# A two-layer graph network on one Trainium2 core: the last groups of the second layer in steps of their own, a first layer drained in smaller portions, and three stores moved behind the tables

## The chip, the cores and the metric

The kernel runs on one core of one Trainium2 chip. The metric is the device time of one execution in microseconds (us). A core has five engines that each run their own list of instructions: PE (TensorE, matrix products; its loads of weights are listed as PEld), DVE (VectorE), ACT (ScalarE), POOL (GpSimd) and SP (SyncE). They wait for each other through semaphores. In this kernel SP only starts DMA transfers, and POOL only starts indirect ones: gathers of rows, and a few scattered stores at the end.

## The reference, cut to what matters

There are 6250 nodes with 256 features and 200000 edges, sorted by destination; each edge has 128 attributes.

```python
# layer 1
e = edge_attr @ W_edge + b_edge
msg = relu(x[src] + e)
agg = segment_sum(msg, dst)
h = relu((x + agg) @ W1 + b1) @ W2 + b2
h = relu((h - mean(h, 0)) * rsqrt(var(h, 0) + 1e-5) * gamma + beta)   # statistics over all nodes
x = layernorm(x + h)
# layer 2: attention with 4 heads
z = einsum('nd,hdf->nhf', x, W)
e = leaky_relu((z . a_src)[src] + (z . a_dst)[dst], 0.01)
e = where(e == 0, -1000, e)
ex = exp(e - segment_max(e, dst)[dst])
out = segment_sum(ex / segment_sum(ex, dst)[dst] * z[src], dst)
x = layernorm(x + out)
```

The statistics of layer 1 run over all nodes, so all of layer 1 must be done before the middle part starts, and the gathers of layer 2 read a table that the middle part writes.

## The kernel before, in words

The edges are cut into 1563 tiles of 128, and these into G = 112 groups: 111 groups of 14 tiles and the last, number 111, of 9 tiles. A group covers at most 128 destination nodes, so sums over edges are matrix products with one-hot matrices (a row for each edge, a column for each node of the group). The program is a straight line: Python loops write out every instruction, and within a manual schedule the order written is the order in which DVE, PE, ACT and SP run their lists. There is no planner.

**Layer 1** (to about 2389 us) goes through 782 pairs of tiles. For pair k it starts the gather of pair k+3 on POOL (L658), adds gathered rows to the products of edge attributes (`sums`, DVE, L672), splits the relu into two parts (`upper`, ACT, L677; `lower`, DVE, L681) and adds pair k-2 into its group's accumulator on PE (`add_up`, L691). When a group's last pair has been added, a generator `flush` takes the group out: `totals` (L526 to L545: add the nodes' own features, two transposes on PE, the copy `hw` on ACT, a carry to the next group), then `mlp` (L408 to L424: product, relu on ACT, product, copies of `h2T` on ACT) and `part_stats` (L433 to L442: masked sums `pmk` on DVE, squares on ACT). Even groups below 110 do only `totals`; the odd ones then run one `mlp` for two groups. Groups 110 and 111 have one each. Each `yield` of the generator gives a number of pairs to wait before its next stage is written; `drive` (L729) moves the active generators once in each step. A negative number means that the next stage may only go when its group is the oldest active one. From group 109 on (`hurry`) `drive` writes two stages in each step instead, without waits. What is still active after the last pair is driven to its end, and then the statistics are merged (L503, L470).

**Middle** (2389 to 2467 us): 14 chunks of nodes, the first of 384, then 512 each, and two of 128. For each chunk: normalise, relu, add x (`add_x`, L860 on; it then stores the features `hn` to `hT_tab`, L863, on SP), products, and `tables_out`, which stores the rows that layer 2 gathers (`z_tab`, L926, SP). `dst_table` stores a second table, `ed_tab` (L933, SP), in two halves, the second at the very end. The buffers of the middle part, those of `hn` among them, are given back before layer 2; layer 2's `ring` lies in that space.

**Layer 2** (2467 to 4965 us) is a loop over steps i (L1243). A step starts the gather of group i+1 (POOL, L1022), loads for group i+3 (L1032, L1034, SP), a load of a group's features (`load_h`, L1047, SP), and then weaves several groups at different ages:

- `logits(i)` (L1102 on, DVE): scans of group i's logits, whose ends go to PE as transposes (`tr`).
- `rows_between` (L1120 on, DVE): maxima across rows of edges, then transposes (`bk`) on PE.
- `maxima` (L1138 on, DVE, then exp on ACT, `exs`, L1145).
- `weigh` for each pair of tiles: `y` on DVE (L1159) and products with the one-hots into `acc` on PE (L1163).
- `onehots` (L1080, L1086, ACT) and `places` with `dst_parts` (ACT, PE) for groups to come.
- `leave` in five stages: transposes of the features; a copy `ag` of `acc` (ACT, L1177); the carry added to `acc` (DVE, L1186) with the first part of the normalising; statistics of the row; the rest and the store of `out` (SP, L1202; for the last KT groups a scatter on POOL, L1204).

The gathered rows live in a ring of five groups, so the gather of group g can only start when `y` of group g-5 has been made. Which groups are weighed in step i is said by `summed(i)`: i-2 up to the step `turn`; i-2 and i-1 together in step `turn + 1`; i-1 after it. Here `SHORT = 7`, so `turn` is 105 and the double step is 106. A step has the groups of `summed(i - 1)` leave and makes the one-hots of `summed(i + 1)`. Step 111 has an order of its own (L1268 on), and steps 112 and 113 finish the weighing and the leaving of group 111.

Of the kernel before, what the change touches and what calls it, by code (L numbers as in the profile page):

```python
# [35 lines left out]
LOOK = 3  # L36
RING = 5
YB = 8
SHORT = 7
XTB = 4  # L40
FIRST = 384
CH = 512
# [12 lines left out]
def gnn(ctx, tc, io, N, E):  # L55
    nc = tc.nc
    NSUB = -(-E // P)
    gs = group_starts(NSUB)
    G = len(gs) - 1
# [451 lines left out]
    with ExitStack() as st:  # L511
# [38 lines left out]
        room = [0, False]  # L550
# [143 lines left out]
        K = len(pairs_)  # L694
# [4 lines left out]
        with tc.manual_schedule(engines={ET.DVE, ET.PE, ET.Activation, ET.SP}):  # L699
            def run(gen):  # L700
                for _ in gen:
                    pass

            run(positions(0, ldp))
            pieces(0)
            bias_rows(gp.tile([P, TB * D], F32, tag="xr", name="row", bufs=LEAD + (not wide)))
            run(hot(0))
            load_rest()
            XW[0] = window(0)
            if G > 1:  # L710
                pieces(1)

            side = [positions(r, ldp) for r in range(1, len(parts))]
            rest = [first_table()]
            checks = [order(r, ldp) for r in range(len(parts))]
            hots, active, extras = iter(()), [], []
            fill = zeros()
            for f in range(min(LOOK, K)):
                fetch(f)
                features(f)  # L720

            def step(queue):
                while queue:
                    if next(queue[0], True) is None:
                        return True
                    queue.pop(0)
                return False

            def drive(k, hurry):  # L729

                for a in list(active):
                    if k >= a[0] and (a[2] > 0 or active[0] is a):
                        a[2] = next(a[1], 0)
                        if hurry and a[2] > 0 and k < K:
                            a[2] = next(a[1], 0)
                        if a[2] == 0:
                            active.remove(a)
                        else:
                            a[0] = k + (1 if hurry else abs(a[2]))
                            if a[2] < 0:  # L740
                                a[2] = -1

            for k in range(K + 2):
                g = pairs_[min(k, K - 1)][0]
                hurry = room[1] = g >= G - 3
                if k < K and pairs_[k][1] == 0:
                    hots = hot(g + 1) if g + 1 < G else iter(())
                    if g + 2 < G:
                        pieces(g + 2)
                    else:  # L750
                        ahead()
                    if g + 1 < G:
                        XW[g + 1] = window(g + 1)
                    if g == GB - 1:
                        while step(rest):
                            pass
                j = k - firsts_[g] if k < K else 99
                if k + LOOK < K:
                    fetch(k + LOOK)
                if k < K:  # L760
                    sums(k)
                    upper(k)
                    if 1 <= k:
                        lower(k - 1)
                elif k == K:
                    lower(k - 1)
                if k + LOOK < K:
                    features(k + LOOK)
                if k >= 2:
                    add_up(k - 2)  # L770
                    if k - 2 in lasts_:
                        gg = pairs_[k - 2][0]
                        active.append([k + (1 if hurry else 4), flush(gg, ACC.pop(gg), XW.pop(gg)), 1])
                if k == min(2, K - 1):
                    places_rest()
                if k == (31 if G > 8 else 1):
                    run(fill)
                elif 2 <= k < 31 and k % 3:
                    next(fill, None)
                if j >= 1 and k >= 3:  # L780
                    next(hots, None)
                if k < K and pairs_[min(k + 1, K - 1)][0] != g:
                    run(hots)
                drive(k, hurry)
                if room[0]:
                    room[0] -= 1
                    if extras and next(extras[0], True) is not None:
                        extras.pop(0)
                        room[0] = 0
                if len(side) >= len(parts) - 1 or not rest:  # L790
                    step(side)
                if 2 <= k < K and k % 2 == 0:
                    step(rest)
                if g >= GB:
                    step(checks)
                if k < K and g == TG and pairs_[k][1] == 0:
                    while step(side):
                        pass
                    while step(checks):
                        pass  # L800
                    extras = [tables(pps, wk), break_columns(), break_rows(pps, wk)]
                    extras += [place_rows(t0, pps, wk) for t0 in range(0, NSUB, P)]
                    room[0] = 0
                if k == K - 1:
                    ahead()
                if k >= K - 19:
                    next(early, None)
            run(early)
            while active:
                k += 1  # L810
                drive(k, True)
            for q in (side, rest, checks, extras):
                while step(q):
                    pass
# [3 lines left out]
    def middle(h2T, stats, ahead=()):  # L818

        with ExitStack() as st:  # L820
# [38 lines left out]
            def add_x(ci):  # L859
                c0, c1 = cs[ci]  # L860
                hn = M["hn", ci][:, :, :c1 - c0]
                nc.vector.tensor_tensor(hn, hn, M.pop(("xt", ci)), op=OP.add)
                nc.sync.dma_start(hT[:, :, c0:c1], hn)  # L863

            def square(ci, k):
                c0, c1 = cs[ci]
# [61 lines left out]
            def dst_table(b0, b1):  # L928

                e7 = zp.tile([P, b1 - b0, EW], F32, name=f"e7_{b0}")  # L930
                nc.vector.tensor_copy(e7[:, :, EW - 1], r_all[:, b0:b1])
                split3(e7.bitcast(BF16)[:, :, :3 * H].rearrange("p b (h c) -> p b h c", c=3), e_all[:, b0:b1], zp)
                nc.sync.dma_start(ed_tab[b0 * P:b1 * P].rearrange("(b p) d -> p b d", p=P), e7)  # L933

            nch = len(cs)
            half = nch // 2

            def at(f, i, *args):
# [3 lines left out]
            with tc.manual_schedule(engines={ET.DVE, ET.PE, ET.Activation, ET.SP}):  # L942
# [13 lines left out]
                for i in range(nch + 3):  # L956
# [16 lines left out]
                    if i - 3 == half:  # L973
                        dst_table(0, cs[half][1] // P)
                dst_table(cs[half][1] // P, NB)

    rest_ = ExitStack()
    rest_.enter_context(tc.manual_schedule(engines={ET.DVE, ET.PE, ET.Activation, ET.SP}))
# [4 lines left out]
    with ExitStack() as st:  # L983
# [228 lines left out]


        turn = max(0, G - SHORT)

        def among(gg):
            return [g for g in gg if 0 <= g < G]

        def summed(i):
            return among([i - 2] if i <= turn else [i - 2, i - 1] if i == turn + 1 else [i - 1])  # L1220

        def run(gen):
            for _ in gen:
# [8 lines left out]
        with tc.manual_schedule(engines={ET.DVE, ET.PE, ET.Activation, ET.SP}):  # L1232
# [10 lines left out]
            for i in range(G + 2):  # L1243
                work = summed(i)
                units = [(g, *u) for g in work for u in pairs(g)]
                hots = [onehots(g) for g in summed(i + 1)]
                outs = [leave(g) for g in summed(i - 1) if ("acc", g) in T]
                parts_, spots = iter(()), []
                if i + 1 < G:
                    gather(i + 1)  # L1250
# [2 lines left out]
                    spots = [places(i + 3)]  # L1253
                if i < G:
                    load_pen(i)
                for g in work:
                    load_h(g)
                    maxima(g)
                if i + 2 < G:
                    parts_ = dst_parts(i + 2)  # L1260
# [4 lines left out]
                        if parts:  # L1265
                            next(parts_, None)

                if i == G - 1 and i > turn + 1:  # L1268

                    some(2)  # L1270
                    logits(i)
                    step(outs)
                    step(hots)
                    some(2)
                    step(hots)
                    rows_between(i)
                    step(outs)
                    some(1)
                    step(hots)
                    step(outs)  # L1280
                    while units or hots:
                        some(1)
                        step(hots)
                    step(outs)
                    out = outs
                    continue
                while out:
                    step(out)
                if i + 1 < G:
                    breaks(i + 1)  # L1290
                step(outs)
                for g in among([i - 1] if i <= turn else []):
                    rows_between(g)
                step(spots)
# [19 lines left out]
                some(1)  # L1314
                while outs:
                    step(outs)
                while units or hots:
                    some(1)
                    step(hots)
                    if len(work) > 1 and not out and len(units) < 4 and ("acc", work[0]) in T:  # L1320
                        out = [leave(work[0])]
                    step(out)
# [221 lines left out]
```

## Time and profile before

| what | value |
|---|---|
| median of 7 runs | 4987.55 us (4973.74 to 4994.21) |
| the runs | 4973.74, 4974.01, 4978.93, 4987.55, 4988.18, 4988.72, 4994.21 |
| the profiled execution's own time | 4977.61 us |
| its span | 4975.8 us, 1.8 us less than its time |
| PE, DVE, ACT, POOL busy | 61%, 55%, 53%, 60% of the span |
| last gather of layer 1; merge of statistics | 2339.2 us; 2389.1 us |
| first gather of layer 2; end of the last gather | 2467.6 us; 4895.7 us |
| last store | 4964.39 us, 0.99 us long |

The span runs from the first instruction to the last in the trace of one execution; times in the trace are counted from its start. A row such as `L1022 POOL DMA_INDIRECT ring<-z_tab,src_sb x1563` names the line of the kernel, the engine, the operation, what is written from what, and how often. In the timeline the first two columns are the start and the busy time in us; a bracket gives the idle time of the engine just before the instruction and the instruction that ended it. The clock given is the one granted to PE, as a share of full speed.

### The profile page before, as it was taken

The numbers are of one execution on the slowest core, as the hardware profiler recorded it, in microseconds if no ns is written. First come the engines' busy times: TensorE is split into PE (matmuls) and PEld (weight loads), VectorE is DVE, ScalarE is ACT, GpSimd is POOL, SyncE is SP. The second block draws the span as 40 slices with busy tenths as digits, with TensorE's granted clock in tenths as the row PEclk, the third lists the DMA queues.
The fourth block names the chain that finished last, engine by engine and source line by source line (L and its number), as shares of the span: only waits on it lengthen the run. The fifth ranks groups of instructions, "written<-read, shape, count | busy, mean of one in ns | idle before, by whom it ended". The sixth has DMA issues, their size and how long they took to land. (4 is left out here: it accounts for less than half of the span.)

```text
span 4975.8 us, 49102 instructions
## 1 busy us (share of the span) xinstructions
PE 3059.0 (61%) x11779; PEld 2185.5 (44%) x11779; DVE 2733.3 (55%) x7689; ACT 2614.5 (53%) x6723; POOL 2965.7 (60%) x3132
## 2 busy tenths in 40 slices
PE   6766667666666666666525555555555555555555
PEld 3555555555555555555413333333333333333333
DVE  5655555555555555555525555555555555555556
ACT  4555555555555555555525545555555555554554
POOL 6666666666666666664165566555665666656552
PEclk8988888888888888888757666666767767666667
DMA  7544444444444444443634444444444444444442
GB/s 256 161 142 139 143 141 140 139 136 136 138 139 140 139 139 139 139 139 113 187 107 112 121 123 120 121 121 116 126 121 116 124 124 123 119 121 126 119 114 57
DMA packets 296691, 656.24 MB, mean 132 GB/s; under 512 B 87274, under 2 KB 158553, under 8 KB 296394
## 3 DMA queue, kind: packets, MB, share of 16 engines
q0 software_dynamic: 150144, 416.54, 30.1%
q1 hardware_dynamic: 144650, 235.43, 15.0%
q8 instruction: 98, 1.61, 0.1%
q14 instruction: 199, 1.63, 0.1%
q10 hardware_dynamic: 1600, 1.04, 0.1%
HBM read 617.82 MB, written 34.99 MB: 131 GB/s over the span
## 5 line engine op out<-in xcount | busy, mean ns | idle before, releaser
L1022 POOL DMA_INDIRECT ring<-z_tab,src_sb x1563 | 1478.9, 946 | 1077.6 <-issue 373.2
L658 POOL DMA_INDIRECT xg<-xb_tab,src_sb x1451 | 1372.5, 946 | 801.0 <-DVE pt L672 398.8
L1163 PE MATMUL acc<-y,oh 128*128 128x260 f32 x3126 | 1171.6, 510 | 658.6 <-issue 382.7
L668 PE MATMUL pt<-we_sb,ea_t 128*128 128x256 f32 x3126 | 1010.0, 454 | 712.7 <-DVE hl L681 540.6
L1163 PEld LDWEIGHTS acc<-y,oh 128*128 128x128 f32 x3126 | 691.5, 243 | 921.0 <-issue 501.8
L668 PEld LDWEIGHTS pt<-we_sb,ea_t 128*128 128x128 f32 x3126 | 677.7, 228 | 939.0 <-issue 789.7
L672 DVE TENSOR_TENSOR pt<-pt,xg 128x512 f32<-128x512 f32 x782 | 542.9, 694 | 941.5 <-remote 746.4
L677 ACT ACTIVATE hl<-pt 128x512 fp32r<-128x512 f32 x782 | 467.4, 598 | 978.3 <-DVE pt L672 818.2
L691 PE MATMUL acc<-hl,oh 128*128 128x512 f32 x1563 | 736.1, 556 | 0.5 <-DVE hl L681 0.5
L681 DVE SCALAR_TENSOR_TENSOR hl<-pt,hl 128x512 fp32r<-128x512 f32 x782 | 533.0, 682 | 7.1 <-ACT hl L677 6.4
L1159 DVE TENSOR_TENSOR y<-ring,exs 128x520 f32<-128x520 f32 x782 | 503.8, 680 | 9.1 <-ACT exs L1145 5.5
L634 ACT ACTIVATE oh<-consts,dloc 128x128 fp32r<-128x128 f32 x1549 | 507.0, 392 | 0.0
L1080 ACT ACTIVATE oh<-consts,dloc 128x128 f32<-128x128 f32 x1563 | 479.2, 388 | 0.0
L691 PEld LDWEIGHTS acc<-hl,oh 128*128 128x128 f32 x1563 | 348.5, 223 | 64.2 <-DVE hl L681 1.1
L1053 ACT ACTIVATE ohT<-dlb,niota 128x1792 bf16<-128x1792 bf16 x112 | 199.4, 1780 | 173.9 <-DMA dlb<-dl_tab 92.9
L1073 PEld LDWEIGHTS <-ohT 128*128 128x128 bf16 x1563 | 160.8, 115 | 272.6 <-issue 191.1
L1186 DVE TENSOR_TENSOR acc<-acc,cr 1x260 f32<-1x260 f32 x111 | 47.1, 424 | 393.0 <-ACT ag L1177 291.0
L1173 ACT COPY pcs<-pc 1x260 f32<-1x260 f32 x111 | 40.1, 361 | 411.5 <-remote 215.6
L1073 PE MATMUL pds<-edw,ohT 128*128 128x12 bf16 x1563 | 149.7, 177 | 102.4 <-issue 99.0
L1086 ACT ACTIVATE oh<-oh 128x896 f32<-128x896 f32 x224 | 208.7, 932 | 4.1 <-issue 3.3
L640 ACT ACTIVATE oh<-oh 128x896 fp32r<-128x896 f32 (+1 forms) x222 | 209.1, 942 | 0.0
L1056 ACT ACTIVATE ohT<-ohT 128x1792 bf16<-128x1792 bf16 x112 | 189.5, 1692 | 3.6
(227 smaller groups left out, 3125.5 us busy)
## 6 DMA issues: line engine op xcount, KB each, us to landing
ea_t<-in_eaT SPq DMA_DIRECT2D x110, 896.0 KB
dlb<-dl_tab SPq DMA_DIRECT2D x111, 448.0 KB
ring<-z_tab,src_sb POOLq DMA_INDIRECT x1563
xg<-xb_tab,src_sb POOLq DMA_INDIRECT x1451
xw<-in_x SPq DMA_DIRECT2D x112, 128.0 KB
hw<-hT_tab SPq DMA_DIRECT2D x112, 128.0 KB
out<-o SPq DMA_DIRECT2D x110, 128.0 KB
z_tab<-zt SPq DMA_DIRECT2D x11, 528.0 KB
```

What stands on the lines that cost most here:

```text
L634: nc.scalar.activation(oh[:, i], iota_r, AF.Square, bias=dloc[:, gs[g] + i:gs[g] + i + 1], scale=-1.0)
L658: nc.gpsimd.indirect_dma_start(out=XG[k][:, i, :], out_offset=None, in_=io["x"] if g < GB else xb_tab, in_offset=bass.IndirectOffsetOnAxis ...
L668: nc.tensor.matmul(pt[:, i, :], EA.pop(gs[g] + j0 + i), we_sb, start=not g < GB, stop=(not g < GB or i == w - 1))
L672: nc.vector.tensor_add(PT[k][:, :w], PT[k][:, :w], XG.pop(k)[:, :w])
L677: nc.scalar.activation(HL[k][:, :w, 0], PT[k][:, :w], AF.Relu)
L681: nc.vector.scalar_tensor_tensor(HL[k][:, :w, 1], PT.pop(k)[:, :w], 0.0, HL[k][:, :w, 0].bitcast(F32), op0=OP.max, op1=OP.subtract)
L691: nc.tensor.matmul(ACC[g].rearrange("p a d -> p (a d)"), OH[g][:, j0 + i], hl[:, i].rearrange("p a d -> p (a d)"), start=(j0 + i == 0), st ...
L1022: nc.gpsimd.indirect_dma_start(out=zg[:, j, :], out_offset=None, in_=z_tab, in_offset=bass.IndirectOffsetOnAxis(ap=src_sb[:, t:t + 1], axi ...
L1073: nc.tensor.matmul(pd[:, j].rearrange("p h c -> p (h c)"), ohT[:, j * P:(j + 1) * P], T["edw", g].bitcast(BF16)[:, :3 * H], start=True, st ...
L1080: nc.scalar.activation(oh[:, i], iota_r, AF.Square, bias=dloc[:, gs[g] + i:gs[g] + i + 1], scale=-1.0)
L1159: nc.vector.tensor_tensor(y[:, :w], T["zg", g][:, j0:j0 + w, :ZW].rearrange("p s (h f) -> p s h f", f=F + 1), by_edge(T["ex", g], g)[:, j0 ...
L1163: nc.tensor.matmul(T["acc", g].rearrange("p h f -> p (h f)"), T["oh", g][:, j0 + i, :], y[:, i].rearrange("p h f -> p (h f)"), start=(j0 + ...
```

## The change

The change has four parts.

1. `SHORT` goes from 7 to 9: `turn` is 103, and the step that weighs two groups is 104 (groups 102 and 103). From step 105 on group i-1 is weighed.
2. A new constant `flat` = 108. Step 108 weighs group 107 and after it group 108, whose `maxima` stands between the two; group 107 leaves beside the weighing of 108. In steps 109, 110 and 111 a group has its logits, rows between, maxima and all its weighing in one step, while the group before it leaves. Group 111 leaves in step 112. One-hots for two groups are now made in step 103 and in step 107 (before: in step 105). The order that step 111 had of its own is gone.
3. `drive` has other portions: from group 104 on, waits of the generators are halved (rounded up); from group 109 on, a stage is written for each pair, with no doubling; group 110's generator has a list of how many stages to write in its first four turns, [1, 2, 4, 3], which a negative wait or the end of the generator cuts short.
4. The stores of the last three chunks' features (512, 128 and 128 nodes, 768 KB) are written behind the last table's store instead of inside `add_x`.

```diff
-SHORT = 7
+SHORT = 9
...
-            def drive(k, hurry):
+            def drive(k, g):
                 for a in list(active):
                     if k >= a[0] and (a[2] > 0 or active[0] is a):
-                        a[2] = next(a[1], 0)
-                        if hurry and a[2] > 0 and k < K:
+                        for _ in range(a[3].pop(0) if a[3] else 1):
                             a[2] = next(a[1], 0)
+                            if a[2] == 0 or a[2] < 0 and active[0] is not a:
+                                break
                         if a[2] == 0:
                             active.remove(a)
                         else:
-                            a[0] = k + (1 if hurry else abs(a[2]))
-                            if a[2] < 0:
-                                a[2] = -1
+                            a[0] = k + (1 if g >= G - 3 else (abs(a[2]) + 1) // 2 if g >= G - 8 else abs(a[2]))
...
-                hurry = room[1] = g >= G - 3
+                room[1] = g >= G - 8
...
-                        active.append([k + (1 if hurry else 4), flush(gg, ACC.pop(gg), XW.pop(gg)), 1])
+                        active.append([k + (1 if g >= G - 3 else 4), flush(gg, ACC.pop(gg), XW.pop(gg)), 1,
+                                       [1, 2, 4, 3] if gg == G - 2 else []])
...
-                nc.sync.dma_start(hT[:, :, c0:c1], hn)
+                if ci < nch - 3:
+                    nc.sync.dma_start(hT[:, :, c0:c1], hn)
+                else:
+                    last_h.append((c0, c1, hn))
...
                 dst_table(cs[half][1] // P, NB)
+                for c0, c1, hn in last_h:
+                    nc.sync.dma_start(hT[:, :, c0:c1], hn)
...
         turn = max(0, G - SHORT)
+        flat = max(turn + 3, G - 4)
...
         def summed(i):
-            return among([i - 2] if i <= turn else [i - 2, i - 1] if i == turn + 1 else [i - 1])
+            return among([i] if i > flat else [i - 2] if i <= turn else [i - 2, i - 1] if i == turn + 1 else [i - 1])
+
+        def all_summed(i):
+            return summed(i) + among([i] if i == flat else [])
...
-                hots = [onehots(g) for g in summed(i + 1)]
-                outs = [leave(g) for g in summed(i - 1) if ("acc", g) in T]
+                hots = [onehots(g) for g in all_summed(i + 1)]
+                outs = [leave(g) for g in all_summed(i - 1) if ("acc", g) in T]
...
-                for g in work:
+                for g in all_summed(i):
                     load_h(g)
+                for g in work if i <= flat else []:
                     maxima(g)
...
+                if flat < i < G:
+                    logits(i)
+                    step(spots)
+                    step(outs)
+                    step(hots)
+                    step(outs)
+                    rows_between(i)
+                    step(spots)
+                    step(outs)
+                    step(hots)
+                    maxima(i)
+                    step(outs)
+                    while units or hots or outs:
+                        some(1)
+                        step(outs)
+                        step(hots)
+                    for _ in parts_:
+                        pass
+                    continue
...
-                while units or hots:
+                if i == flat:
+                    some(len(units))
+                    for g in among([i]):
+                        maxima(g)
+                        units = [(g, *u) for u in pairs(g)]
+                    out = [leave(g) for g in work]
+                while units or hots or i == flat and out:
                     some(1)
                     step(hots)
```

## The prediction

> **What bounds the kernel now.** I read the page's first two parts, then the chain of waits, then the windows and the timeline of the two places that the change touches. The chain that ended last is cut short by the profiler (all of its rows say 0%), so the wait view and the timeline stand in for it.
>
> ```profile
> span 4975.8 us, 49102 instructions
> PE 3059.0 (61%) x11779; PEld 2185.5 (44%) x11779; DVE 2733.3 (55%) x7689; ACT 2614.5 (53%) x6723; POOL 2965.7 (60%) x3132
> ...
> POOL 6666666666666666664165566555665666656552
> PEclk8988888888888888888757666666767767666667
> ...
> L1022 POOL DMA_INDIRECT ring<-z_tab,src_sb x1563 | 1478.9, 946 | 1077.6 <-issue 373.2
> ```
>
> No engine is full over the whole span, so each stage has its own limit. In layer 2 gathers leave POOL every 946 + 300 ns (timeline), 17.5 us for 14 tiles, and POOL still waits 279.6 us for `y` to free the ring:
>
> ```profile
> POOL ring L1022 <- DVE y L1159: 279.6, 98, 11.7
> ...
> POOL ring L1022 <- DMA ed_tab<-e: 127.5, 1, 127.5
> ```
>
> By windows, its end has two parts (columns: window, length, then busy time and count of PE, PEld, DVE, ACT, POOL, granted clock, DMA share, GB/s):
>
> ```profile
> 4850.00:4875.00 25.00, 11.11 (x47) 7.50 (x47) 7.23 (x18) 2.64 (x6) 18.90 (x20) 0.75 0.51 138
> 4875.00:4900.00 25.00, 17.81 (x66) 10.27 (x66) 18.96 (x66) 13.78 (x37) 10.68 (x11) 0.70 0.31 85
> 4900.00:4925.00 25.00, 19.04 (x88) 12.77 (x89) 21.86 (x70) 18.64 (x55) 0.00 (x0) 0.86 0.09 25
> 4925.00:4950.00 25.00, 18.98 (x76) 12.50 (x74) 23.19 (x78) 13.26 (x42) 0.00 (x0) 0.93 0.09 22
> ```
>
> Until 4895.7 gathers run, and steps come in two lengths: 12.85 us, or some 13 us more when all engines crawl beside the gathers (from 4857 to 4877 single matmuls stand about 2.2 us apart). After that DVE is 87 to 93% busy: the tail is bound by DVE, with 5 us of idle time in these 50. The starts of its steps are the first `maxima` lines:
>
> ```profile
> 4910.18 0.16 DVE L1138 TENSOR_TENSOR top<-top,trbk 128x8 f32<-128x8 f32 x1
> 4923.02 0.16 DVE L1138 TENSOR_TENSOR top<-top,trbk 128x8 f32<-128x8 f32 x1
> 4935.84 0.16 DVE L1138 TENSOR_TENSOR top<-top,trbk 128x8 f32<-128x8 f32 x1
> 4964.39 0.99 POOL L1204 DMA_INDIRECT out<-o,oidx  x1 [5.23 <-ACTq L1468]
> ```
>
> These lines are 12.84 and 12.82 us apart. Step 108, the start of which I call S, has its line at 4896.0; the last store follows at S+68.4.
>
> **The change part by part.** The profiled execution took 4977.61 us, its span 4975.8 and 1.8 around it. It belongs to the lower of two bunches of the seven runs (three from 4973.74 to 4978.93, four from 4987.55 to 4994.21). Their distance, about 13 us, is one crawling step. The median, 4987.55, is 9.9 above the profiled run. I work out the change against 4977.61 and add 9.9, assuming that the bunches mix as before.
>
> *A: the turn comes two steps earlier (the double step is 104, not 106).* From the start of step 104 to the end of step 107 the same five groups (102 to 106) are weighed before and after, and gather(111) waits for `y` of group 106, in step 107 both times. So S depends on the same work: zero, give or take one crawl, 13 us. `load_h` on SP and the stores of `out` move with their steps; SP waits there for the ring of gathered rows no more than before. New is a second set of one-hots in step 107: 14×0.30 + 2×0.93 = 6.1 us of ACT, beside 18.64/25×12.85 = 9.6 us: 15.7 in a step of 12.85, so +2.8 if the step is undisturbed, 0 if it crawls. I take +2. Beyond it the bounds are −22.5 (step 106 took 48.2 us, from 4834.2 to 4882.4, against 2×12.85) and +13.
>
> *B: step 108 takes two groups, and 109 to 111 are flat: logits, maxima and weighing of one group in the same step.* Removed are the last step's latency and nothing of the work of DVE. Added is a serial loop: logits, transposes on PE behind the matmuls of the group before, `rows_between`, the first part of `leave` (the add to `acc`), `maxima`, exp, first `y`. From one first `y` to the next: `y` 0.69 + 28 matmuls 7.15 at full clock + transposes 0.3 + `rows_between` 1.16 + stage 3 of `leave` 2.51 + `maxima` 1.08 + exp 0.22 = 13.1 us at the least. PE then starts after a gap of 6 us or more, and after gaps of half that size the first pair ran at half clock:
>
> ```profile
> 4907.20 2.10 PE L1163 MATMUL acc<-y,oh 128*128 128x260 f32 x4 [3.22 <-DVE y L1159]
> 4910.22 1.25 PE L1163 MATMUL acc<-y,oh 128*128 128x260 f32 x4
> ```
>
> At half clock for the 3.4 us that such stretches last in the windows, 6.7 matmuls run instead of 13.3: +1.65. Exp stands on ACT behind four one-hots (1.26), and stage 4 or its transposes add some 0.6: 16.6. Group 109's first `y` came at S+28.3; now logits 1.95, `rows_between` 1.16 and `acc` 1.49 stand in front: S+32.9. Two loops: S+66.1. Group 111 has 9 tiles: 18 matmuls 4.6 + 1.65, then 5.2 from `acc` to the store and 1.0 for it: S+78.5, that is +10. Least: loops of 13.1 and a warm last group give S+69.9, +1.5, and I use +4 as nearest to the row at 4907.20, which shows that some cold start is sure. Most: +15, with another 1.65 in each of three steps. A gain is possible only out of those 5 us of DVE's idle time; I keep −2 as the far end.
>
> The Trainium skill, "TensorE: Matmul & The Clock Gate", section "What's actually happening", speaks against this part: an idle window of about 3.4 us halves the clock, and about as much sustained work is needed to win it back. The trace agrees in size (3.4 us at 0.5 after each gap of the tail). By the rule every flat step starts cold, as I count it; if only the shorter gaps did, B would be about 5 less.
>
> *C: the first layer's way out.* Groups 104 to 108 have their waits halved, from 109 on one stage per pair instead of two, and group 110 gets the list [1,2,4,3]. Before, the hurried stages made DVE stand still while ACT was behind:
>
> ```profile
> 2342.93 0.29 DVE L436 SCALAR_TENSOR_TENSOR pmk<-p,mk 128x128 f32<-128x128 f32 x1 [3.30 <-ACT h2T L424]
> ...
> 2365.32 0.29 DVE L436 SCALAR_TENSOR_TENSOR pmk<-p,mk 128x128 f32<-128x128 f32 x1 [3.31 <-ACT h2T L424]
> ...
> 2377.31 0.48 DVE L526 SCALAR_TENSOR_TENSOR ag<-xw,opem,acc 128x256 f32<-128x256 f32 x1 [0.72 <-PE acc L691]
> 2380.78 0.35 ACT L533 COPY hw<-acc 128x256 f32<-128x256 f32 x1
> ```
>
> Last gather was at 2339.2, so from there on every stall of DVE is on the path. With the 1.78 at 2326.69 the stalls are 8.4 us. Late next: group 109's mlp now ends one pair behind the last, and 110's first product waits for it (stages marked negative go in order), so part of 110's mlp goes behind the last pair. Its chain from the `hw` copy at 2373.96 to `pmk` at 2378.92 is 5.0 us, and the last group's own `hw` copy stood 2.1 us behind that work already. I take −6. Ends: −10 (8.4 and most of the 2.1), and +3 (no stall cured and 110's chain starting at 2377.3 instead of 2374.0).
>
> *D: the last three stores of features (768 KB) go behind the tables on SP.* Layer 2's first gather waited for the tables:
>
> ```profile
> 2460.63 0.40 SPq L933 DMA_DIRECT2D ed_tab<-e  x1
> 2467.59 0.95 POOL L1022 DMA_INDIRECT ring<-z_tab,src_sb  x1 [127.49 <-DMA ed_tab<-e]
> ```
>
> It also needs the space of the features' buffers, for the ring lies there, so it waits for the moved stores. They cannot leave before about 2461.1, 0.45 each on SP, and the loads of step 0 get 1.4 us later, hidden behind the gathers. At the 187 to 256 GB/s of the two busiest slices 768 KB take 3 to 4 us; landing costs about 2 (a store issued at 2457.79 landed at 2459.76). Free engines would give 2467: nothing. But the last 106 rows of `z_tab` took from 2460.03 to 2466.76 on two engines; behind those it is 3.5 more. Ends 0 and +6. The tables do not leave sooner: their stores follow their own copies on ACT, not the queue. I take +3.5, as the row of 106 rows is in the way for certain. First gather and end shift one for one, since gathers 0 to 4 run alone after it.
>
> The Trainium skill, "DMA: Bandwidth & Descriptors", section "Why a DMA increments its semaphore by 16 and not by 1", has a store's rows shared by the largest number up to 16 that divides its partitions, which for 106 gives the two engines seen. A store of 128 rows would then also have a sixteenth on each of these two, and by that D is 3.5, not 0.
>
> Sum: 2 + 10 − 6 + 3.5 = +9.5. Against the profiled run 4987.1, against the median 4997.
>
> **The rivals.** What repeated timing can tell from no change is about 0.2%, 10 us: below 4977.6 is faster, above 4997.5 slower.
>
> - *The double step's stall goes (other side).* Step 106 held 22.5 us of crawl. If the groups weighed two steps earlier free the ring so that the gathers are over before the loads of step 107 come, this doesn't return: 4997 − 22.5 = 4974.5. For: POOL waited 7.04 us for `y` at 4881.73, and from 4769.8 to 4895.7 gathers of 98.7 us fill 126. Against: the crawl follows loads beside gathers, and as many of those remain. It decides from 19.5 us.
> - *One more crawl.* The double step falls into another phase of loads and gathers: 4997 + 13 = 5010. The two bunches of runs speak for such a step, its equal work against it.
> - *Nothing left of the losses.* PE is warm (B +4), the features land beside the tables (D 0), A 0: −2, 4985.5. For: DMA share was 0.04 from 2459 to 2461. Against: the two-engine row.
> - *The way out isn't shortened.* 110's chain behind the last pair costs what the stalls gave, C +3: 5006. For: stages in order. Against: the 3.3 us stalls are ACT's doing and go with the doubling.
>
> **How the numbers follow.** Forecast 0.42, its own range 4989 to 5003 (B from +4 to +15, mostly); stall gone 0.15; one more crawl 0.16; nothing left 0.20; way out 0.07. The forecast sits at the bound, so I split it 0.22 same and 0.20 slower. Faster 0.15; same 0.22 + 0.20 = 0.42; slower 0.20 + 0.16 + 0.07 = 0.43. Leaving out half of each outer case, the range runs from 4974 to 5012.
>
> **What would show it.** A: step 107's crawl or length, and the last gather near 4895.7 + shift. B: first `y` of 109, 110, 111 some 16 us apart, DVE below 80% in the flat steps. C: statistics (L503) near 2383 and the 3.3 us stalls gone. D: first gather at 2471 less C's gain. Wrong would make it: a first gather no later than the tables, loops of 13 us, or a different number of crawling steps near the end.

## The result, and the profile after

The changed kernel takes 5002.34 us (median of 14 runs, 4985.85 to 5015.21), the kernel before 4983.62 us (35 runs, 4967.42 to 4995.09). The ratio is 1.0041, with a 95% interval of 1.003 to 1.0051: some 20 us slower. The profiled execution has a span of 5004.6 us, 28.8 more than before. The two profiled executions thus lie further apart than the medians (18.7) or the ratio (20.4): executions of one and the same kernel spread by 28 us here (4967.42 to 4995.09 before). What follows explains this pair of executions; the ratio tells what the change costs.

The work is the same; only idle time has been added (first parts of the page):

```profile
span 5004.6 us, 49102 instructions
PE 3058.3 (61%) x11779; PEld 2191.6 (44%) x11779; DVE 2731.8 (55%) x7689; ACT 2612.9 (52%) x6723; POOL 2966.4 (59%) x3132
```

Four places of the trace show where the 28.8 us come from.

**The first layer's way out.** The timeline of DVE and ACT at the end of layer 1:

```profile
2344.24 0.29 DVE L436 SCALAR_TENSOR_TENSOR pmk<-p,mk 128x128 f32<-128x128 f32 x1 [0.58 <-ACT h2T L424]
...
2364.46 0.29 DVE L436 SCALAR_TENSOR_TENSOR pmk<-p,mk 128x128 f32<-128x128 f32 x1
...
2372.36 0.29 DVE L436 SCALAR_TENSOR_TENSOR pmk<-p,mk 128x128 f32<-128x128 f32 x1 [3.78 <-ACT h2T L424]
...
2381.51 0.18 DVE L503 COPY st_eq<-g_sq 128x16 f32<-128x16 f32 x1 [0.41 <-ACT pmk L442]
```

The two stalls of 3.3 us are gone (0.58 is left of them). One of 3.78 us is new: group 110's, which now stands behind the last pair, so that the last group's way from `ag` to the merge takes 14.1 us (2367.46 to 2381.51) instead of 11.8. The merge of the statistics is at 2381.51, before at 2389.12: 7.6 us earlier.

**The moved stores.** SP and POOL at the end of the middle part:

```profile
2454.15 0.39 SPq L937 DMA_DIRECT2D ed_tab<-e  x1
2454.58 4.66 SPq L982 DMA_DIRECT2D hT_tab<-hn  x3
...
2464.78 0.94 POOL L1029 DMA_INDIRECT ring<-z_tab,src_sb  x1 [125.62 <-DMA hT_tab<-hn]
```

The releaser in the last bracket was `ed_tab` and is now `hT_tab`: the first gather waits for the moved stores. It follows the issue of the last table's store by 10.6 us instead of 7.0. Of the 7.6 us 2.8 are left (2464.78 against 2467.59); the other 1.1 passed between the merge and that store. The view's `ed_tab` is an inference. The trace's semaphores say more: before, POOL's wait ended at 2466.79, when the store of the 106 rows had landed (2466.76), and `ed_tab` landed only at 2468.02, after the gather had begun. After the change the 106 rows had landed at 2460.38 and the last of the moved stores at 2463.86, 3.5 us later; POOL's wait ended at 2463.90.

**The turn.** Windows of steps 103 to 107, in which groups 101 to 106 are weighed, first of before, then of after (columns as in the prediction's windows):

```profile
4769.80:4782.50 12.70, 11.36 (x54) 7.72 (x54) 11.91 (x38) 10.84 (x27) 7.31 (x8) 0.84 0.33 83
4782.50:4809.70 27.20, 13.27 (x44) 7.48 (x43) 12.01 (x39) 11.54 (x28) 15.63 (x18) 0.59 0.39 109
4809.70:4834.20 24.50, 11.77 (x54) 7.79 (x53) 12.99 (x44) 11.74 (x29) 13.28 (x15) 0.71 0.40 108
4834.20:4882.40 48.20, 24.86 (x93) 16.17 (x93) 20.38 (x61) 18.69 (x49) 28.96 (x31) 0.71 0.44 120
4882.40:4896.00 13.60, 11.25 (x42) 6.23 (x42) 12.67 (x44) 11.88 (x30) 9.37 (x11) 0.75 0.38 100
```

```profile
4774.30:4798.80 24.50, 11.46 (x53) 7.64 (x52) 12.98 (x44) 11.74 (x29) 13.27 (x15) 0.71 0.39 108
4798.80:4847.10 48.30, 25.44 (x93) 16.27 (x93) 20.50 (x62) 18.68 (x49) 29.05 (x31) 0.71 0.45 120
4847.10:4860.60 13.50, 10.85 (x48) 6.53 (x47) 12.57 (x44) 11.88 (x30) 9.28 (x11) 0.87 0.36 100
4860.60:4888.60 28.00, 12.57 (x44) 7.13 (x43) 12.14 (x40) 11.65 (x28) 15.14 (x17) 0.63 0.38 104
4888.60:4912.90 24.30, 11.42 (x51) 8.04 (x50) 12.08 (x40) 11.65 (x28) 11.99 (x13) 0.71 0.39 109
```

Both double steps take 48 us, and both are followed by a short step of 13.5. Before, the gathers were over with that short step (the last one starts at 4895.7 and ends at 4896.6), and in these traces no step without gathers crawls. After the change two more steps with gathers follow, and both crawl: 138.6 us instead of 126.2, with 70.3 us of DVE work in it against 70.0.

The two traces enter step 103 at different places of the rhythm, though. Ahead of the turn one step in three is short; step 103 is the short one before, and a long one after. Counted from the start of step 101, both took 179 us to the start of step 108 (179.1 and 178.6). So this pair alone does not price the turn. The last experiment brings a trace of the old order that enters step 103 as the changed kernel does.

**The tail.** From the start of step 108 (4912.9) to the last store:

```profile
4919.51 0.70 DVE L1166 TENSOR_TENSOR y<-ring,exs 128x520 f32<-128x520 f32 x1 [5.53 <-ACT exs L1152]
...
4950.13 2.10 PE L1170 MATMUL acc<-y,oh 128*128 128x260 f32 x4 [2.41 <-DVE y L1166]
4952.12 2.08 PE L1170 MATMUL acc<-y,oh 128*128 128x260 f32 x4
4954.09 2.08 PE L1170 MATMUL acc<-y,oh 128*128 128x260 f32 x4
...
4960.66 0.42 DVE L1193 TENSOR_TENSOR acc<-acc,cr 1x260 f32<-1x260 f32 x1 [4.25 <-ACT ag L1184]
...
4993.59 0.99 POOL L1211 DMA_INDIRECT out<-o,oidx  x1 [11.05 <-ACTq L1486]
```

It is 80.7 us long, before it was 68.4. The first `y` of groups 107 to 111 stand at 6.6, 19.4, 36.5, 53.3 and 67.7 us after the start of step 108, before at 1.3, 15.5, 28.3, 41.1 and 53.3.

Together: 2.8 earlier at the first gather, 19.7 lost between it and step 108 (7.3 of them before step 103, in code that the change doesn't touch; 12.4 from step 103 on), 12.3 in the tail: 29.2 later at the last store.

### The profile page after: what moved, and what is told of

The parts are those of the page before. It is cut to its first block, busy times and chain, and to the rows that moved or that the text cites. A ratio compares the mean times of both kernels' runs of the same rounds, so it can differ in the third digit from the quotient of the medians.

```text
span 5004.6 us, 49102 instructions
## 1 busy us (share of the span) xinstructions
PE 3058.3 (61%) x11779; PEld 2191.6 (44%) x11779; DVE 2731.8 (55%) x7689; ACT 2612.9 (52%) x6723; POOL 2966.4 (59%) x3132
```

## The experiments

The chips matter here. On some, the kernel before takes some 4980 us, as in the runs above, with crawling steps; on others 4080 us, with none. Three chips were of the second kind and one of the first, each met once; the chip of the runs above is not on record. Each ratio below is against the kernel before on the same chip. All kernels but the last of this section ran on chips of the 4080 us kind.

**The way out alone.** `drive`, `room[1]` and the list as in the change; the old loop of layer 2 and the stores inside `add_x`. Against the whole change:

```diff
-SHORT = 9
+SHORT = 7
...
-                if ci < nch - 3:
+                if ci < nch:
```

> Only part C (the first layer's way out). Theory 1 (each part acts in its own place and the parts add up): the merge of statistics stands 7.6 us earlier, as in the two traces (2389.12 against 2381.51), layer 2's first gather as much earlier (near 2460.0), and the time falls by 7 to 8 us: ratio about 0.9985. Rival (what layer 2 gets early it loses again, since its steps come in a rhythm of 12.85 us and crawls, and the end falls on a step of that rhythm): first gather 7.6 us earlier, but the time within 3 us of before: ratio 0.9995 to 1.0005.

Measured: 4071.71 against 4080.66 us, ratio 0.9978 (0.9969 to 0.9987): 9 us faster. The first gather stood at 2063.98. In the kernels of the same chip with the old way out it stood at 2076.9 and 2077.1, 13 us later; the merge was 10.7 to 11.5 us later there (1997.95 and 1998.81 against 1987.30). Theory 1 holds in kind, and the gain is somewhat larger than in the first pair of traces.

**The stores alone.** On the kernel before:

```diff
-                nc.sync.dma_start(hT[:, :, c0:c1], hn)
+                if ci < nch - 3:
+                    nc.sync.dma_start(hT[:, :, c0:c1], hn)
+                else:
+                    last_h.append((c0, c1, hn))
...
                 dst_table(cs[half][1] // P, NB)
+                for c0, c1, hn in last_h:
+                    nc.sync.dma_start(hT[:, :, c0:c1], hn)
```

> Only part D (the last three stores of features behind the tables). Theory 1: the first gather is released by the moved stores and comes 3.7 us later after the last table's store than before (10.6 against 7.0 us), so near 2471.3; the time grows by 3 to 4 us: ratio about 1.0007. Rival (the stores are hidden by what the first gather waits for anyway): first gather within 1 us of 2467.6 and no change of time.

Measured: 4082.48 against 4080.66 us, ratio 1.0007 (0.9998 to 1.0016). The time alone decides nothing, but the trace does: the last table's store was issued at 2070.13 and the first gather came 9.9 us later; with the way out alone, whose stores are where they were, it was 6.3 (2057.66 to 2063.98). The stores cost 3.5 us of delay at the first gather, and the rival falls: 106 rows landed at 2075.34, the last moved store at 2079.09.

**The turn alone.** On the kernel before:

```diff
-SHORT = 7
+SHORT = 9
```

> Only part A (the double step is 104 instead of 106; the tail of before is kept). Theory 1: the same five groups are weighed between the start of step 104 and the end of step 107, 113.5 us before and 114.1 after the whole change, so time within 3 us of before: ratio 0.9995 to 1.0005. Rival (the turn itself brings a crawl in most runs, which would explain the some 10 us of the whole change's 20 that the other parts leave open): 8 to 13 us more, ratio 1.0016 to 1.0026, and more than 113.5 us between those two places.

Measured: 4081.47 against 4080.66 us, ratio 1.0000 (0.9991 to 1.0009). Here the double step took 26.3 us (3919.3 to 3945.6), not 48, and no step crawled. Where nothing crawls, the turn costs nothing that can be told (interval −3.7 to +3.7 us). Of the chips where steps crawl this run says nothing.

**The flat steps alone.** The new loop of layer 2 with the old turn; the way out and the stores as before. Against the whole change, besides undoing those two parts:

```diff
-SHORT = 9
+SHORT = 7
```

> Only part B (step 108 takes two groups, 109 to 111 are flat; the double step stays 106). Theory 1: from the start of step 108 to the last scatter 80.7 us as after the whole change, against 68.4 before: 12 us more, ratio about 1.0025; the first y of step 108 waits some 5.5 us for the exponential behind the one-hots of two groups on ACT, and the flat groups' first y stand 14 to 17 us apart. Rival (the whole change's tail was long because of where the turn put it, not because of the flat steps): tail within 4 us of 68.4 and the time within 4 us of before.

Measured: 4085.29 against 4080.66 us, ratio 1.0010 (1.0001 to 1.0019): 4.6 us slower. From step 108 to the last store 78.8 us. The wait of 5.5 us was there (first `y` 6.6 us after the start of the step), and the flat groups' first `y` stood 15.3 and 15.2 us apart. But the three kernels with the old tail took 76 to 78 us for it on this chip, where the last gather came 45 to 47 us after the start of step 108. So the tail was nearly as long as expected, but its price was not 12: 4.6 us by the medians (0.4 to 7.8 by the ratio's interval), 0.6 to 3.0 between the traces. The likely reason is that the old tail waits for gathers here and is longer for it; the runs without the last gathers, further down, test that.

**The whole change, and turn with flat steps, side by side.** The second has `drive` and its calls as before, and the stores inside `add_x`:

```diff
-            def drive(k, g):
+            def drive(k, hurry):
...
-                if ci < nch - 3:
+                if ci < nch:
```

> The whole change once more, beside single parts on one chip. Theory 1 (the parts add up): where the gathers run back to back and nothing crawls, way out −9, stores +3, turn +1, flat +5: together 0, ratio 0.9995 to 1.0003. Where steps of layer 2 crawl: −8, +4, 0 and +12, so some 8 us more, ratio 1.0016. Rival (what layer 2 gains early is lost in its rhythm of crawling steps, or the parts disturb each other): ratio near 1.004 again where steps crawl, and there alone.

> Parts A and B together, without the way out and without the moved stores. Theory 1: turn 0 and flat +5 without crawls, 0 and +12 with them: ratio 1.001 or 1.0025. Rival (the earlier turn and the flat tail are made for each other and the tail gets shorter): ratio below 1.0.

Measured: the whole change 4076.39 against 4080.71 us, ratio 0.9989 (0.9980 to 0.9998): 4 us faster. Turn and flat steps 4084.09 us, ratio 1.0006 (0.9997 to 1.0015). The single parts add up to −9.0 + 1.8 + 0.8 + 4.6 = −1.8 us, inside the interval of the whole (−8.2 to −0.8). So the same change is a little faster on a chip where nothing crawls, and 0.4% slower on one where steps crawl. The second kernel had no shorter tail (80.4 us), so the rival falls.

**The way out with smaller last tables.** The 106 rows and the second half of `ed_tab` in smaller stores:

```diff
-                        nc.sync.dma_start(z_tab[z0:z1].rearrange("(b p) d -> p b d", p=n), zt[:n, b0:b0 + nbz, :])
+                        for p0, p1 in ((0, n // 16 * 16), (n // 16 * 16, n)) if nbz == 1 else ((0, n),):
+                            if p1 > p0:
+                                nc.sync.dma_start(z_tab[z0:z1].rearrange("(b p) d -> p b d", p=n)[p0:p1],
+                                                  zt[p0:p1, b0:b0 + nbz, :])
...
+                    if i - 3 == nch - 3:
+                        dst_table(cs[half][1] // P, cs[nch - 3][1] // P)
-                dst_table(cs[half][1] // P, NB)
+                dst_table(cs[nch - 3][1] // P, NB)
```

> The way out (part C) alone, and beside it the last tables' stores cut smaller: the 106 rows of z_tab as 96 and 10 rows, and the second half of ed_tab in two stores, of which the last holds only the two last chunks. Nothing else is left out or moved. Theory 1 (the first gather waits for the last ed_tab store and the 106-row store, 7.0 us after the issue of the first): the first gather follows the last table's store by 3 to 4 us instead of 7, and the time falls by 8 to 9 us for the way out and 3 more for the stores: ratio 0.997 without crawls, 0.998 with them. Rival (the stores' landing time is not a matter of their size or their engines): first gather still 6 to 7 us behind, ratio as for the way out alone, 0.9978.

Measured: 4069.83 against 4080.71 us, ratio 0.9970 (0.9959 to 0.9980). The first gather did follow the last table's issue by 4.2 us (2060.74 to 2064.98) instead of 6.3, but that issue came later after the merge (73.4 us against 70.4), since one more `dst_table` and more stores stand in front. From the merge to the first gather it was 77.6 us, with the way out alone 76.7: nothing gained. The interval overlaps that of the way out alone, so the difference of the two is not told by these runs.

**What the flat steps cost where the gathers are over.** The first profile's tail is bound by computing. To have that on a chip where nothing crawls, four kernels leave out the gathers of the last five groups:

```diff
-            for j, t in enumerate(groups(g)):
+            for j, t in enumerate(groups(g) if g < G - 5 else []):
```

The first is the kernel before, the second has the flat steps with `SHORT = 7`. The third makes the one-hots of group 108 in step 108:

```diff
-                hots = [onehots(g) for g in all_summed(i + 1)]
+                hots = [onehots(g) for g in (among([i]) if i == flat else []) + summed(i + 1)]
```

The fourth has the second's order and keeps PE busy:

```diff
+        def warm_up(n):
+            for _ in range(n):
+                nc.tensor.matmul(trbk[:, 384:512], ident, ident, start=True, stop=True)
...
+                    warm_up(10)
                     rows_between(i)
+                    warm_up(10)
```

> The kernel before without the gathers of the last five groups (their rows are whatever the ring still holds, so what these groups put out has no meaning): the tail is then bound by computing, also where nothing crawls. A yardstick for the three others. Theory: from the start of step 108 to the last scatter 68 us, as in the first profile, where the gathers were over by then.

> Part B alone (double step 108 and flat steps), again without the gathers of the last five groups. Theory 1 (the flat steps cost 12 us where the gathers are over, and only 5 where the tail waits for gathers, because the wait covers the rest): 80 us from step 108 to the last scatter, 11 to 13 us more than the yardstick. Rival (the crawling execution alone made the tail long): 3 to 5 us more, as with the gathers.

> As the one before, but the one-hots of group 108 are made in step 108 instead of step 107. Theory 1 (at the start of step 108 the exponential stands 5.5 us behind the one-hots of two groups on ACT): first y of step 108 1.3 us after its start instead of 6.6, and the end 3 to 5 us earlier than the flat kernel with early one-hots. Rival (the one-hots are then missed later, in front of the second half's matmuls): within 1 us of it, with PE waiting for ACT in step 108.

> Part B without the last five gathers, and 20 products of the unit matrix with itself (128 columns each, into columns that nothing reads) on PE in every flat step, before and behind the transposes of rows_between, so that PE doesn't idle between two groups. Theory 1 (half the price of the flat steps is the half clock after PE's gap: 3 of the 7 pairs took 2.1 us instead of 1.0): the pairs of groups 109 to 111 take 1.0 to 1.25 us each and the end is 4 to 7 us earlier than without the products. Rival (the products stand in the way of the transposes, or the clock falls all the same): within 1 us, or later.

| without the last five gathers | median us | first `y` of 107, 109, 111 after the start of step 108 | last store after it |
|---|---|---|---|
| kernel before | 4073.63 | 1.3, 28.0, 53.0 | 68.0 |
| flat steps | 4085.46 | 6.6, 36.5, 67.3 | 80.3 |
| flat, one-hots of 108 in step 108 | 4083.03 | 1.3, 32.4, 64.8 | 76.9 |
| flat, PE kept busy | 4089.36 | 6.6, 38.5, 73.6 | 85.5 |

All four ran on one chip. Lines of the first two's timelines, the last store of each and the wait at step 108 of the flat one:

```profile
4059.14 0.99 POOL L1204 DMA_INDIRECT out<-o,oidx  x1 [5.23 <-ACTq L1468]
```

```profile
4001.33 0.70 DVE L1165 TENSOR_TENSOR y<-ring,exs 128x520 f32<-128x520 f32 x1 [5.53 <-ACT exs L1151]
...
4074.96 0.99 POOL L1210 DMA_INDIRECT out<-o,oidx  x1 [10.96 <-ACTq L1485]
```

Flat steps cost 11.8 us in the medians and 12.3 in the traces, as in the first pair of profiles (12.3). This settles the tail: its price is the flat order itself, and neither the crawling nor the turn. Moving the one-hots takes the wait of 5.5 us away, but only 2.4 us of the median and 3.3 of the trace come back: 109's first `y` is 4.1 earlier, and from there the flat steps lose part of it again. The intervals of the two ratios overlap, so the gain in time is not certain.

With PE kept busy the trace's clock stays at half for 3.4 us in each flat step, not for 6.8 to 10.2. So a shorter gap does leave PE at the full clock for longer, as the rule of the Trainium skill that the prediction cites ("TensorE: Matmul & The Clock Gate", section "What's actually happening") has it. But the half clock did not go: single pairs still took up to 2.0 us. And the kernel got slower, by 3.9 us in the medians and 5.3 in the traces. Each ten products took some 2.4 us, and DVE's `rows_between` and `maxima` waited for them:

```profile
4036.24 2.40 PE L1234 MATMUL trbk<-consts 128*128 128x128 f32 x20
4038.68 0.47 DVE L1126 TENSOR_TENSOR_SCAN down<-pen,down,trbk 4x128 f32<-4x128 f32 x1 [0.77 <-PE trbk L1234]
...
4040.05 2.50 PE L1234 MATMUL trbk<-consts 128*128 128x128 f32 x20
4042.58 0.17 DVE L1144 TENSOR_TENSOR top<-top,trbk 128x8 f32<-128x8 f32 x1 [1.67 <-PE trbk L1234]
```

So the first half of its rival holds and the second in part, and what a warm PE would be worth by itself is not measured.

**The way out alone, where steps crawl.** The same kernel as the first, on a chip of the 4980 us kind.

> Part C alone once more, as the version that beats both kernels so far. Theory 1: 8 to 10 us less than the kernel before, ratio about 0.998, on this chip too, and from the first gather to the start of step 108 as long as before. Rival (where steps of layer 2 crawl, an early start of layer 2 is lost again before its end): ratio 0.9995 or more if the kernel before takes some 4980 us here.

Measured: 4971.78 against 4980.04 us, ratio 0.9987 (0.9974 to 0.9999), some 6.5 us faster. The first gather stood at 2458.67, 8.9 us earlier than in the first profile of before. In its one profile 6.4 us of that were lost by the start of step 108 (2434.8 us after the first gather instead of 2428.4), as the rival has it; the ratio of all runs is better than the rival's bound of 0.9995, but the interval reaches beyond it, so theory and rival are not told apart by time. Its tail was 12 us shorter than that of the whole change, as it should be with the old order. Steps 103 to 107 took 25.5, 12.8, 29.1, 48.2 and 13.5 us: 129.1, near the 126.2 of before and not the 138.6 after the change. Here the short step of the rhythm is 104, where the changed kernel has its double step:

```profile
4764.30:4789.80 25.50, 12.41 (x55) 8.17 (x55) 11.89 (x40) 12.03 (x29) 16.70 (x18) 0.77 0.55 153
4789.80:4802.60 12.80, 11.81 (x55) 8.14 (x55) 12.01 (x39) 10.85 (x27) 7.40 (x8) 0.78 0.30 81
```

## Why the prediction was right, and where its terms were off

The direction and the range were right: slower, 5002.34 inside 4974 to 5012. The forecast was 9.5 us above the kernel before, and the measured ratio makes it 20.4: twice as much. That 5002 lies just inside the forecast's own range (4989 to 5003) is luck: the kernel before took 3.9 us less than in the first seven runs, and its 35 runs fill the stretch from 4967 to 4995 without the two bunches read from seven. Above the old median the result would stand at 5008, in the part of the range that only the rivals "one more crawl" and "the way out isn't shortened" had opened. By terms:

| part | predicted | where steps crawl | where none does |
|---|---|---|---|
| A, the turn | +2 | +9.5 to +12.4 (three traces) | +0.8 |
| B, double step 108 and flat steps | +10 | +12.3 (traces) | +4.6; +11.8 without the last gathers |
| C, way out | −6 | −6.5 (ratio); −7.6 (trace) | −9.0 |
| D, stores behind the tables | +3.5 | +3.7 (traces) | +1.8; 3.5 in the trace |
| sum | +9.5 | +19.0 to +21.9 | −1.8 |
| the whole change | +9.5 | +20.4 | −4.3 |

**A is the term that was mis-sized.** The prediction put it at +2, with the argument that "the same five groups (102 to 106) are weighed before and after" between the start of step 104 and the end of step 107. That stretch was equal indeed, 113.5 and 114.1 us. But equal work was counted from a point that has itself a place in the rhythm of short and crawling steps. Among steps 103 to 107 both traces of the old order have two short steps, the new order has one. Against the old order that enters step 103 in the same place of the rhythm (138.6 against 129.1) this is 9.5 us; against the first trace (126.2), which enters it in another place, 12.4. That is the rival "one more crawl", priced at 13, which came in kind for this term. Taking B, C and D as measured from the ratio's 20.4 leaves 10.9, so the size fits. It is read from three traces where steps crawl, and from the turn alone (26.3 us for the double step, no loss) where none does. The turn alone did not meet a chip where steps crawl, so it is not isolated: a loss that comes only with the other parts is not excluded.

**B** was right in mechanism and low. The prediction set S+78.5 against S+68.4, but the first includes 1.0 us of the last store itself and the second does not; by its own terms B is +9.1, and measured 12.3. Group 109's first `y` was put at S+32.9 and came at S+36.5. Missing was the exponential that waits 5.5 us on ACT behind the one-hots of two groups: the prediction had these one-hots under A, as an overflow of step 107, and the exponential of the next step paid for them. With the one-hots moved (the third kernel without the last gathers) that `y` came at S+32.4. The two loops were put at 16.6 each and took 16.8 and 14.4, 2.0 less in sum. Their cold start was right on average, and uneven: 28 matmuls, put at 8.8 us, took 10.1 in group 109 (4950.13 to 4960.22) and 7.9 in group 110 (4966.91 to 4974.84), and 8.5 and 8.8 in the flat steps alone. The end after the last first `y` was put at 11.4 up to the store and took 13.0. So +3.6 − 2.0 + 1.6 make the 3.2 us that were missing. That the tail is bound by DVE was true of before only: in the two loops DVE was 70 and 74% busy (4954.0 to 4970.4 and on to 4985.0), and it waited 4.25 us at 4960.66 for `ag`, the copy of `acc` that follows PE's matmuls.

**C** was put at −6 and measured −6.5 to −9. The stalls of DVE did go, and the counterweight was there as predicted: group 110's mlp behind the last pair, a new stall of 3.78 us.

**D** was put at +3.5 and came out at 3.7. The Trainium skill, "DMA: Bandwidth & Descriptors", section "Why a DMA increments its semaphore by 16 and not by 1", gave the prediction its reason why the moved stores would be held up: 106 rows are shared by two engines, and a store of 128 rows has a sixteenth on each of these two. The trace agrees on the two engines (two landing marks, 2459.64 and 2460.38), but not on the hold-up. If two engines were late, two of the sixteen marks of each moved store would be late. All sixteen lie within 0.8 us (2462.53 to 2463.29, 2462.83 to 2463.51, 2463.16 to 2463.86), and the first of them 2 us behind the 106 rows. What the trace shows instead is that the first of the three stood 3.2 us on SP (2454.58 to 2457.79) where a store of its size mostly takes 0.46, and that the `ed_tab` store ahead of it landed from 2460.58 to 2462.72. So the size was right, and the step behind it is not what the marks show. Why SP held that store so long stays open.

The rival that ends on the other side, the double step's stall going away, did not come: the double step took 48.3 us, as before. On the chips where nothing crawls it has no object. "Nothing left of the losses" fell with B and D, "the way out isn't shortened" with C.

The version to keep is the way out alone: 0.9978 and 0.9987 against the kernel before, on the two kinds of chips. With the smaller last tables it was 0.9970, on one kind only and not told apart from the other.

## What to carry to other kernels

A step of a tail that does everything for one group in a row saves one step of latency and pays, in every step, the matmuls of the group that the next one has to wait for: 12 us over four groups here, of which a tail that waits for transfers hides more than half. When work is moved within a rhythm of short and long steps, the sum must be made from a point at the same place of the rhythm ahead of it to a fixed point behind it; the same groups in the same number of steps can still hit one long step more. And a store moved out of the way of another is only out of the way if nobody waits for its buffer: the next stage's first gather did.

## What the runs showed of the hardware that was not expected

The same kernel takes 4980 us on some chips and 4080 on others. The gathers take 946 to 951 ns in both, and the middle part 79 us. Layer 1 differs: its last gather starts at 2339 us on the former and at 1966 on the latter. So does layer 2, whose steps take about 17.6 us on the latter (14 gathers of 1.25 us), and for long stretches 27.2, 25.6 and 12.8 in turn, 21.9 on average, on the former. The mean granted clock is 0.77 on the former and 0.85 to 0.86 on the latter; whether that is a cause or follows from PE's longer gaps is not shown. Busy time of DVE in a step is the same, 12 us. In a crawling step the engines wait for nothing that the profile shows, as in the trace of before:

```profile
4862.79 0.59 PE L1163 MATMUL acc<-y,oh 128*128 128x260 f32 x1 [2.59 <-issue]
4864.92 0.59 PE L1163 MATMUL acc<-y,oh 128*128 128x260 f32 x1 [1.54 <-issue]
```

Single matmuls of 0.59 us start 2.1 to 2.8 us apart, and the profile names nothing that they wait for. What holds their issue up on these chips stays open; no experiment here touched it.
